# Order of statistics, scaling and stores at the end of a cross-attention and feed-forward kernel

## The chip, the cores and the metric

The kernel runs on one core of a Trainium2 chip. The metric is the device time of one execution in microseconds (us). Engines are called by the profile's names: PE is TensorE (matrix products), DVE is VectorE, ACT is ScalarE, POOL is GpSimd, SP is SyncE, which here only issues transfers. SBUF is the core's working memory, PSUM the memory of eight banks that PE writes its products to.

## The reference

The inputs are x (4 batches of 2048 tokens, 512 features, fp32), a context of 77 keys for each batch, two gates and the weights. Cut to what matters:

```python
x = x + tanh(g_xattn) * (softmax(q(layernorm(x)) @ k.T / 8) @ v @ Wo + bo)   # 16 heads
x = x + tanh(g_ffn) * (layernorm(x) @ W[idx] + b[idx])                        # idx chosen by argmax
```

The second line concerns us here. The product of a centred weight with the not yet normalized row is scaled afterwards by the row's 1/sqrt(var + eps), so the norm's statistics are needed only when the product is scaled, not before it is made. The result is y plus bias plus scaled product.

## The kernel before

The 8192 tokens are worked in 16 groups of 512. For each group there are scores, softmax, the attention's product (`at`), a residual sum in columns (features on partitions), a change of layout to rows of y, and the feed-forward product `ff`. Each 512 x 512 product is made in seven block products instead of eight (class `Seven`): `product(s)` issues the matmuls of step s into one of three PSUM banks, `post(s)` copies the bank to the SBUF tile `snap` (ACT, L467) or adds it there (DVE, L486). Sums of column blocks that these products read (`T1` to `T4`, `Columns.sum`) are made on POOL (L432).

The schedule is manual: each engine works its instructions in the order in which the code issues them, and waits between engines come from the data they share. The tracking goes by whole banks in PSUM.

In rows, a group's y is a tile of 128 partitions x 16 row blocks x 128 features. `stats` makes statistics of it on DVE (L365), `gather` has ACT bring them to 32 partitions in 8 copies (L374), half of them to PSUM (`ps_st`), `calc` works the variance out in seven DVE instructions (L381 to L388), `power` takes it to the power -1/2 on POOL (L393), and `back` copies the result to all four quarters of the partitions as `rs` (L398).

The last group has no later work to hide behind, so it is worked in halves and quarters. The last four of its 128-feature columns of blocks are named by two indices: `h` is the half of the features, `v` the half of the tokens (rows 8v to 8v+7 of y). `n1` holds the statistics of tokens half v=1 (the second half), `n0` those of v=0 (the first). Each quarter of the product goes through the same steps: finished in `snap` (or, for h=1, v=0, left in the bank `ff.ps[0]`), transposed to rows in the tile `t` by two DVE transposes (`f_rows`, `to_rows`, L412), scaled by `rs` (L996 on ACT block by block, L1000 at once on DVE or POOL), and added to y (L1004). The bias is added to y by halves on POOL (`half_bias`, L991). `store` (L594) writes half the tokens by four transfers of 128 KB, on the queues it is given.

In the loop over the last product's steps, s is the step: after step 3 quarter (h, v) = (0, 1) is complete, after step 4 (1, 1), after step 5 (0, 0), after step 6 (1, 0). The order before, by engine, behind the last attention product: DVE makes rows and statistics for v=1, the last rows of x, `n1.calc`, rows and statistics for v=0, then the adds and transposes of step 3, `n0.calc`, and so on; the four copies `n0.back` are on DVE:

```python
            n0.back(nc.vector.tensor_copy)
            scaled_at_once(0, 0, n0.rs, nc.gpsimd)
            added(0, 0, nc.gpsimd)
```

PSUM tiles come from `bank()`, a pool of seven buffers; the statistics have the eighth bank, `stat`.

Of the kernel before, what the change touches and what calls it, by code (L numbers as in the profile page):

```python
# [11 lines left out]
ALU = mybir.AluOpType  # L12
# [7 lines left out]
def flamingo_block_kernel(  # L20
# [33 lines left out]
    nc = tc.nc  # L54
# [9 lines left out]
    NA = 4  # L64
# [10 lines left out]
    NG = T // 32  # L75
# [12 lines left out]
    def bank(name):  # L88
        return pm.tile([P, 512], F32, tag="mm", name=name)
# [22 lines left out]
    stat = pst.tile([P, 512], F32, tag="st", name="ps_st")  # L112
# [19 lines left out]
    def row_tile(name):  # L132
        return wp.tile([P, NG, P], F32, tag="row", name=name, bufs=3)
# [9 lines left out]
    t = wp.tile([P, NK * T + KH * T2], F32, tag="pT", name="wq")  # L143
# [3 lines left out]
    xg, ys, ts_ = {}, {}, {}  # L147

    def rows_of(t, i):
        return t[ts(i, T), :].rearrange("(g c) d -> c g d", c=32)  # L150
# [91 lines left out]
    def gather():  # L242
        t = row_tile("wfr").rearrange("p g j -> p (g j)").rearrange("p (c d) -> p c d", c=NDC)
        for c in range(NDC):
            at = bass.IndirectOffsetOnAxis(ap=rows_u[:, c : c + 1], axis=0)
            nc.gpsimd.indirect_dma_start(out=t[:, c, :], out_offset=None, in_=W, in_offset=at)
        at = bass.IndirectOffsetOnAxis(ap=rows_u[:, NDC:], axis=0)
        nc.gpsimd.indirect_dma_start(out=bf_r, out_offset=None,
                                     in_=b.rearrange("o (a j) -> (o a) j", j=P), in_offset=at)
        nc.gpsimd.tensor_scalar(bo_c, bo_c, tgx, None, ALU.mult)  # L250
        nc.gpsimd.tensor_scalar(bf_r, bf_r, tgf, None, ALU.mult)
        return t
# [100 lines left out]
    class Norms:  # L353
# [10 lines left out]
            for g in range(g0, g0 + n):  # L364
                nc.vector.bn_stats(self.s6[:, at + g, :], t[:, g, :])  # L365

        def gather(self):

            self.mean = stat[:32, : 8 * self.n].rearrange("p (n e) -> p n e", e=2 * NA)
            self.m2 = small.tile([32, self.n, 2 * NA], F32, tag="m2", name="m2")  # L370
            parts = self.s6.rearrange("p g (h s) -> p g h s", h=2)
            for a in range(NA):
                for to, k in ((self.mean, 1), (self.m2, 2)):
                    nc.scalar.copy(to[:, :, ts(a, 2)], parts[ts(a, 32), :, :, k])  # L374
# [34 lines left out]
    def to_rows(dst, cols, q, v=None):  # L409

        g = slice(0, NG) if v is None else ts(v, NG // 2)
        nc.vector.transpose(dst[:, g, ts(q, 32)], cols.rearrange("p (g c) -> p g c", c=32))  # L412
# [81 lines left out]
    norms, xc, yc, sc, pT = ({} for _ in range(5))  # L494
# [51 lines left out]
    def p_columns(i, k0, k1):  # L546
        for k in range(k0, k1):
            if k == 0:
                t = wp.tile([P, NK * T + KH * T2], F32, tag="pT", name="pT")
                pT[i] = Columns(t[:, : NK * T].rearrange("p (n t) -> p n t", t=T),  # L550
                                T1=t[:, NK * T :].rearrange("p (n t) -> p n t", t=T2))
            nc.vector.transpose(pT[i].all[:, k, :].rearrange("p (g h r) -> p g h r", h=HA, r=R),  # L552
                                key_chunk(sc[i], k))

    def residual(j, at, which, engine=None):

        c = xc[j].at["B" + which]
        (engine or nc.gpsimd).tensor_tensor(c, c, at.quarter(which), ALU.add)  # L558

    def residual_last(j, at):  # L560

        c = xc[j].at["B21"]
        for n, pair in enumerate(at.pairs):
            q = pair + NDC // 2
            nc.vector.scalar_tensor_tensor(c[:, n, :], at.ps[0][:, n, :], bo_c[:, q : q + 1], c[:, n, :],
                                           ALU.add, ALU.add)

    def y_rows(j, q0, v=None):
        if j not in ys:
            ys[j] = row_tile("y")  # L570
        for q in (q0, q0 + 1):
            c = xc[j].all[:, q, :]
            to_rows(ys[j], c if v is None else c[:, ts(v, T2)], q, v)

    def f_rows(f, ff, half, v=None):
        if f not in ts_:
            ts_[f] = row_tile("t")
        for n in range(2):
            to_rows(ts_[f], ff.chunk(half, n, v), 2 * half + n, v)

    def add_bias(f, engine):
        engine.tensor_tensor(ys[f], ys[f], bf_r.unsqueeze(1).to_broadcast([P, NG, P]), ALU.add)
# [9 lines left out]
    def store(f, g0=0, n=NG, queues=(nc.sync,)):  # L592
        for a in range(NA):
            queues[a % len(queues)].dma_start(out=rows_of(out, f)[:, ds(g0, n), ts(a, P)],  # L594
                                              in_=ys[f][ts(a, 32), ds(g0, n), :])
# [54 lines left out]
    ff = None  # L650

    def end_of_ff(f):
        ff.product(6)
        ff.post(6)
# [11 lines left out]
    n = norms[0]  # L666
# [67 lines left out]
    e = (8, 16, 24, 32, 41, 50, 57)  # L734
# [47 lines left out]
    for i in range(1, NGRP):  # L782
        j, f, nx = i - 1, i - 2, i + 1
        n = norms[i]
# [67 lines left out]
        for s in range(7):  # L852
# [12 lines left out]
            if 1 <= s:  # L865
                e = (0, 10, 20, 32, 44, 56, 64)
# [44 lines left out]
        ff = Seven("ps_f", w_ffn, yc[j], (0, 1), SNAP)  # L911
        for s in range(6):
# [16 lines left out]
            if 2 <= s:  # L929
                k = (0, 2, 3, 5, 6)  # L930
# [5 lines left out]
    j, f = NGRP - 1, NGRP - 2  # L936
    n = norms[NGRP] = Norms(NGRP)
    n1, n0 = Norms(NGRP + 1, NG // 2), Norms(NGRP + 2, NG // 2)
# [3 lines left out]
    for s in range(7):  # L942
        at.product(s)
        if s == 0:
            at.post(0)
            end_of_ff(f)
            p_columns(j, 6, 10)
            f_rows(f, ff, 1)
            pT[j].sum("T2")
            pT[j].sum("T3")  # L950
            n.stats(ys[f], 0, 0, NG)
        if s == 1:
            n.gather()
            add_bias(f, nc.vector)
        if s == 2:
            n.calc()
            pT[j].sum("T4")
            n.power()
        if s == 3:
            n.back()  # L960
            f_scale(f, n.rs, 0, 8)
        if s == 4:
            residual(j, at, "12")
            f_scale(f, n.rs, 8, 8)
        if 0 < s < 6:
            at.post(s)
        if s == 4:
            f_add(f, 0, NG, nc.vector)
            store(f)
        if s == 5:  # L970
            residual(j, at, "22")
            y_rows(j, 0, 1)
        if s == 6:
            yc[j].sum("T3")
            residual(j, at, "11")
            y_rows(j, 2, 1)
            n1.stats(ys[j], -8, 8, 8)
            n1.gather()
            y_rows(j, 0, 0)
            residual_last(j, at)  # L980
    yc[j].sum("T1")
    yc[j].sum("T2")
    ff = Seven("ps_f", w_ffn, yc[j], (0, 1), SNAP, None, Seven.BY_TOKENS)

    def by_feature(t, h, v):

        return t[:, ts(v, NG // 2), ts(h, D // NA // 2)]

    def half_bias(v, engine):
        y = ys[j][:, ts(v, NG // 2)]  # L990
        engine.tensor_tensor(y, y, bf_r.unsqueeze(1).to_broadcast([P, NG // 2, P]), ALU.add)  # L991

    def scaled(h, v, rs):
        d = by_feature(ts_[j], h, v)
        for g in range(NG // 2):
            nc.scalar.activation(d[:, g, :], d[:, g, :], AF.Copy, scale=rs[:, g : g + 1])  # L996

    def scaled_at_once(h, v, rs, engine):
        d = by_feature(ts_[j], h, v)
        engine.tensor_tensor(d, d, rs.unsqueeze(2).to_broadcast(list(d.shape)), ALU.mult)  # L1000

    def added(h, v, engine):
        y = by_feature(ys[j], h, v)
        engine.tensor_tensor(y, y, by_feature(ts_[j], h, v), ALU.add)  # L1004

    for s in range(6):
        ff.product(s)
        if s == 0:
            half_bias(1, nc.gpsimd)
            n1.calc()  # L1010
            n1.power()
            y_rows(j, 2, 0)
            n0.stats(ys[j], 0, 0, 8)
            yc[j].sum("T4")
            half_bias(0, nc.gpsimd)
        ff.post(s)
        if s == 2:
            n1.back()
            n0.gather()
        if s == 3:  # L1020
            f_rows(j, ff, 0, 1)
            scaled(0, 1, n1.rs)
            n0.calc()
            n0.power()
        if s == 4:
            f_rows(j, ff, 1, 1)
            scaled(1, 1, n1.rs)
            added(0, 1, nc.gpsimd)
        if s == 5:
            f_rows(j, ff, 0, 0)  # L1030
            n0.back(nc.vector.tensor_copy)
            scaled_at_once(0, 0, n0.rs, nc.gpsimd)
            added(0, 0, nc.gpsimd)
    ff.product(6)
    for k in range(2):
        to_rows(ts_[j], ff.ps[0][:, k, :], 2 + k, 0)
    added(1, 1, nc.vector)
    store(j, 8, 8, (nc.sync, nc.sync, nc.sync, nc.scalar))
    scaled_at_once(1, 0, n0.rs, nc.vector)
    added(1, 0, nc.vector)  # L1040
    store(j, 0, 8, (nc.sync, nc.scalar))


# [39 lines left out]
```

## Time and profile before

| what | us |
|---|---|
| median of 3 runs (lowest, highest) | 1262.63 (1260.26, 1262.82) |
| the profiled execution | 1261.98 |
| its span, first to last instruction | 1260.2 |
| PE busy in the span | 1241.3 (99%) |
| DVE busy | 914.0 (73%) |
| POOL busy | 876.8 (70%) |
| ACT busy | 685.6 (54%) |
| PE's last matmul ends | 1249.89 |
| DVE's last add (L1004) ends | 1254.82 |

The span is what the profile's clock covers; the 1.8 us between it and the execution's time lie around it. Busy time is an average over the whole kernel, and the change is in its last 23 us. For them the timeline is read: each line has the start, the length, the engine, the line of the code, the operation with output and inputs, and in brackets how long the engine was idle before it and what ended that.

### The profile page before, as it was taken

What the parts mean: (1) busy time and instruction counts of PE and PEld (TensorE: products, weight loads), DVE (VectorE), ACT (ScalarE), POOL (GpSimd) and SP (SyncE); (2) the same over time, 40 slices, a digit from 0 to 9 for tenths busy, and PEclk for the clock granted to TensorE, in tenths of its full rate; (3) what the DMA queues carried; (4) which work ended last, traced back from release to release, by engine and by line L of the source; (5) the groups of instructions that cost most, each with busy time, mean ns of one, the idle gap of its engine ahead of it and who ended that gap; (6) DMA issues with size and microseconds to landing.
All of it is one profiled execution on the core that took longest, in us unless ns stands there. A gap on an engine that the chain in (4) does not pass through costs nothing.

```text
span 1260.2 us, 16984 instructions
## 1 busy us (share of the span) xinstructions
PE 1241.3 (99%) x5704; PEld 1061.0 (84%) x5704; DVE 914.0 (73%) x1859; ACT 685.6 (54%) x1964; POOL 876.8 (70%) x470
## 2 busy tenths in 40 slices
PE   9989999999999999999999999999999999999996
PEld 6665888888888888888888888888888888888885
DVE  5778876677776767777776877666777876666577
ACT  3547473827456483736548373654738274564823
POOL 4332896685967778584968778575986877585766
PEclk9999999999999999999999999999999999999998
DMA  9775500304006030303206030122304111010102
GB/s 254 293 214 179 147 1 1 68 21 116 15 1 151 1 68 1 67 1 93 58 1 151 1 67 1 26 42 84 67 1 109 43 43 25 1 34 1 34 1 67
DMA packets 95221, 80.27 MB, mean 64 GB/s; under 512 B 3856, under 2 KB 83088, under 8 KB 95136
## 3 DMA queue, kind: packets, MB, share of 16 engines
q1 hardware_dynamic: 92768, 76.74, 23.8%
q0 software_dynamic: 608, 1.13, 0.4%
q10 hardware_dynamic: 1760, 1.34, 0.3%
q8 instruction: 45, 0.74, 0.2%
q14 instruction: 40, 0.33, 0.1%
HBM read 44.07 MB, written 35.13 MB: 63 GB/s over the span
## 4 chain that ended last, share of the span: by engine, by line
PE 93%; POOL 3%; DVE 2%; ACT 1%; DMA 1%; issue 0%; SPq 0%; POOLq 0%; DVEq 0%; ACTq 0%
PE ps_s L461 36%; PE ps_a L461 36%; PE ps_f L461 15%; PE ps_kv L266 2%; PE ps_vo L331 2%; PE ps_m L296 2%; POOL vo L123 1%; DMA xg<-in_x_dram 1%; POOL pT L432 1%; PE ps_w L167 0%; POOL s L543 0%; DVE snap L486 0%; POOL xc L558 0%; ACT wf L644 0%; POOL wf L123 0%
## 5 line engine op out<-in xcount | busy, mean ns | idle before, releaser
L461 PE MATMUL ps_a<-pT,vo 128*128 128x256 f32 x2240 | 486.2, 379 | 0.0
L461 PEld LDWEIGHTS ps_a<-pT,vo 128*128 128x128 f32 x2240 | 425.6, 190 | 57.9
L532 ACT ACTIVATE s<-s,nmx,up 128x77 f32<-128x77 f32 x1024 | 355.6, 446 | 1.0 <-DVE nmx L526 1.0
L432 POOL TENSOR_TENSOR pT<-pT 128x1280 f32<-128x1280 f32 x64 | 185.8, 2905 | 171.5 <-PE ps_a L461 162.0
L461 PE MATMUL ps_s<-tq,m 128*128 128x256 f32 x1280 | 292.4, 381 | 6.5 <-ACT snap L467 5.6
L461 PEld LDWEIGHTS ps_s<-tq,m 128*128 128x128 f32 x1280 | 243.3, 191 | 43.9 <-ACT snap L467 6.4
L467 ACT COPY snap<-ps_s 128x512 f32<-128x512 f32 (+1 forms) x188 | 93.3, 514 | 289.2 <-DVE t L412 131.3
L461 PE MATMUL ps_s<-xc,m 128*128 128x256 f32 x960 | 222.3, 381 | 0.0
L461 PEld LDWEIGHTS ps_s<-xc,m 128*128 128x128 f32 x960 | 182.6, 191 | 29.3 <-DVE vo L334 2.4
L543 POOL TENSOR_TENSOR s<-s,sm 128x1232 f32<-128x1232 f32 x64 | 145.2, 2270 | 64.0 <-DVE sm L540 41.6
L486 DVE TENSOR_TENSOR snap<-snap,ps_s 128x512 f32<-128x512 f32 (+1 forms) x141 | 83.5, 593 | 123.5 <-PE ps_s L461 120.7
L461 PE MATMUL ps_f<-tq,wf 128*128 128x256 f32 x512 | 118.5, 379 | 0.6 <-DVE snap L486 0.4
L552 DVE STREAM_TRANSPOSE pT<-s 128x512 f32<-128x512 f32 x160 | 101.0, 678 | 18.2 <-POOL s L543 18.2
L393 POOL TENSOR_TENSOR r<-r,neghalf 32x16 f32<-32x16 f32 (+1 forms) x33 | 93.1, 2831 | 29.6 <-DVE r L388 29.1
L432 POOL TENSOR_TENSOR tq<-xc,tq 128x512 f32<-128x512 f32 x64 | 85.3, 1333 | 34.8 <-PE ps_f L461 32.3
L461 PEld LDWEIGHTS ps_f<-tq,wf 128*128 128x128 f32 x512 | 97.1, 190 | 14.5 <-issue 0.7
L515 DVE STREAM_TRANSPOSE s<-snap 128x512 f32<-128x512 f32 x156 | 99.8, 685 | 10.1 <-ACT snap L467 7.9
L539 DVE TENSOR_REDUCE sm<-s 128x16 f32<-128x1232 f32 x64 | 91.5, 1430 | 20.8 <-ACT s L532 20.7
L524 DVE TENSOR_REDUCE ps_st<-s 128x16 f32<-128x1232 f32 x64 | 92.4, 1444 | 2.1
L432 POOL TENSOR_TENSOR tq<-xc 128x512 f32<-128x512 f32 x64 | 81.4, 1272 | 13.7 <-DVE xc L407 12.3
L461 PE MATMUL ps_f<-xc,wf 128*128 128x256 f32 x384 | 90.7, 379 | 0.0
L467 ACT COPY snap<-ps_f 128x512 f32<-128x512 f32 x63 | 36.9, 585 | 88.9 <-PE ps_f L461 88.8
(126 smaller groups left out, 1180.3 us busy)
## 6 DMA issues: line engine op xcount, KB each, us to landing
xg<-in_x_dram SPq DMA_DIRECT2D x64, 256.0 KB, 6.2
out_dram<-y SPq DMA_DIRECT2D x60, 256.0 KB, 4.1
vo<-vo_d SPq DMA_DIRECT2D x16, 640.0 KB, 5.5
vo_d<-vo SPq DMA_DIRECT2D x16, 512.0 KB, 3.8
m<-m_d SPq DMA_DIRECT2D x12, 640.0 KB, 4.1
m_d<-vo SPq DMA_DIRECT2D x4, 960.0 KB, 6.1
wq<-in_WqT_dram SPq DMA_DIRECT2D x8, 256.0 KB, 8.0
wq<-in_Wo_dram SPq DMA_DIRECT2D x1, 2048.0 KB
```

Source lines behind the costliest of these rows:

```text
L266: nc.tensor.matmul(ps[:, :n], w[:, c, ts(p, P)], keys[:, c].rearrange("p b j -> p (b j)"), start=(c == 0), stop=(c == NCC - 1))
L393: nc.gpsimd.tensor_tensor(r, r, neghalf[:32, : r.shape[1]], ALU.pow)
L432: (engine or nc.gpsimd).tensor_tensor(self.at[name], self.at[a], self.at[b_], op)
L461: nc.tensor.matmul(self.ps[r][:, n, :], self.w(blk, c, pair), self.cols(cname, c), start=(first and n == 0 and c == 0), stop=(c == h - 1), ...
L467: nc.scalar.copy(dst, self.ps[r])
L486: nc.vector.tensor_tensor(c, c, self.ps[r], ALU.add)
L515: nc.vector.transpose(key_chunk(sc[i], k), cols.rearrange("p (g h r) -> p g h r", h=HA, r=R))
L524: nc.vector.tensor_reduce(mx, head(i, h), AX.X, ALU.max)
L532: nc.scalar.activation(head(i, h)[:, g, :], head(i, h)[:, g, :], AF.Exp, scale=norms[i].up[:, g : g + 1], bias=nmx[h][:, g : g + 1])
L539: nc.vector.tensor_reduce(sm, head(i, h), AX.X, ALU.add)
L543: nc.gpsimd.tensor_tensor(head(i, h), head(i, h), sums[h].unsqueeze(2).to_broadcast([P, NG, J]), ALU.mult)
L552: nc.vector.transpose(pT[i].all[:, k, :].rearrange("p (g h r) -> p g h r", h=HA, r=R), key_chunk(sc[i], k))
```

## The change

Five things change, all in the last group:

1. The rows of y for the first half's second features and the statistics `n0.stats` come directly behind the last residual sum, ahead of `n1.calc`. `n0.gather` comes one step earlier (ahead of ACT's copy of step 2) and writes a bank of its own, `ps_n`; `n0.calc` and `n0.power` follow `n1`'s.
2. On POOL, `T4` goes ahead of `n1.power`, and the bias of the first half behind `n0.power`.
3. Quarter (1, 1) is transposed into a new PSUM bank `ps_r` instead of `t`; half of its blocks are scaled there at once by DVE, the other half by four ACT instructions. Quarter (1, 0) is transposed into another such bank and scaled there at once by DVE. The adds to y read the bank.
4. `n0.back` is on ACT, behind the scaling of quarter (1, 1). The add of quarter (0, 1) on POOL is issued one step earlier.
5. The second half is added to y and its stores issued before the last quarter is transposed; its four transfers alternate between SP and ACT (before: three on SP, one on ACT).

```diff
-        def gather(self):
-            self.mean = stat[:32, : 8 * self.n].rearrange("p (n e) -> p n e", e=2 * NA)
+        def gather(self, bank_=stat):
+            self.mean = bank_[:32, : 8 * self.n].rearrange("p (n e) -> p n e", e=2 * NA)
...
             residual_last(j, at)
+            y_rows(j, 2, 0)
+            n0.stats(ys[j], 0, 0, 8)
...
+    def rows_bank(chunks):
+        d = bank("ps_r").rearrange("p (g j) -> p g j", g=NG // 2)
+        for k in range(2):
+            nc.vector.transpose(d[:, :, ts(k, 32)], chunks[k].rearrange("p (g c) -> p g c", c=32))
+        return d
+
+    def scaled(d, rs, g1=NG // 2):
+        for g in range(g1):
             nc.scalar.activation(d[:, g, :], d[:, g, :], AF.Copy, scale=rs[:, g : g + 1])
+    def scaled_at_once(d, rs, engine, g0=0):
+        d, rs = d[:, g0:], rs[:, g0:]
         engine.tensor_tensor(d, d, rs.unsqueeze(2).to_broadcast(list(d.shape)), ALU.mult)
+    def added(h, v, d, engine):
         y = by_feature(ys[j], h, v)
+        engine.tensor_tensor(y, y, d, ALU.add)

     for s in range(6):
         ff.product(s)
         if s == 0:
             half_bias(1, nc.gpsimd)
+            yc[j].sum("T4")
             n1.calc()
             n1.power()
-            y_rows(j, 2, 0)
-            n0.stats(ys[j], 0, 0, 8)
-            yc[j].sum("T4")
-            half_bias(0, nc.gpsimd)
+        if s == 2:
+            n0.gather(bank("ps_n"))
+            n0.calc()
+            n0.power()
         ff.post(s)
         if s == 2:
             n1.back()
-            n0.gather()
+            half_bias(0, nc.gpsimd)
         if s == 3:
             f_rows(j, ff, 0, 1)
-            scaled(0, 1, n1.rs)
-            n0.calc()
-            n0.power()
+            scaled(by_feature(ts_[j], 0, 1), n1.rs)
+            added(0, 1, by_feature(ts_[j], 0, 1), nc.gpsimd)
         if s == 4:
-            f_rows(j, ff, 1, 1)
-            scaled(1, 1, n1.rs)
-            added(0, 1, nc.gpsimd)
+            r1 = rows_bank([ff.chunk(1, k, 1) for k in range(2)])
+            scaled_at_once(r1, n1.rs, nc.vector, NG // 4)
+            scaled(r1, n1.rs, NG // 4)
+            n0.back()
         if s == 5:
             f_rows(j, ff, 0, 0)
-            n0.back(nc.vector.tensor_copy)
-            scaled_at_once(0, 0, n0.rs, nc.gpsimd)
-            added(0, 0, nc.gpsimd)
+            t = by_feature(ts_[j], 0, 0)
+            scaled_at_once(t, n0.rs, nc.gpsimd)
+            added(0, 0, t, nc.gpsimd)
     ff.product(6)
-    for k in range(2):
-        to_rows(ts_[j], ff.ps[0][:, k, :], 2 + k, 0)
-    added(1, 1, nc.vector)
-    store(j, 8, 8, (nc.sync, nc.sync, nc.sync, nc.scalar))
-    scaled_at_once(1, 0, n0.rs, nc.vector)
-    added(1, 0, nc.vector)
+    added(1, 1, r1, nc.vector)
+    store(j, 8, 8, (nc.sync, nc.scalar))
+    r0 = rows_bank([ff.ps[0][:, k, :] for k in range(2)])
+    scaled_at_once(r0, n0.rs, nc.vector)
+    added(1, 0, r0, nc.vector)
     store(j, 0, 8, (nc.sync, nc.scalar))
```

In the changed kernel the scaling at once is L1008, ACT's scaling L1004, the transposes into a bank L999, the adds L1012 and the bias L993.

More of the change, by code (lines that the diff above doesn't have):

```diff
@@ L991, in half_bias @@
         engine.tensor_tensor(y, y, bf_r.unsqueeze(1).to_broadcast([P, NG // 2, P]), ALU.add)
-    def scaled(h, v, rs):
-        d = by_feature(ts_[j], h, v)
-        for g in range(NG // 2):
+    def rows_bank(chunks):
[5 more added lines that the diff above has]
+        for g in range(g1):
             nc.scalar.activation(d[:, g, :], d[:, g, :], AF.Copy, scale=rs[:, g : g + 1])
-    def scaled_at_once(h, v, rs, engine):
-        d = by_feature(ts_[j], h, v)
+    def scaled_at_once(d, rs, engine, g0=0):
+        d, rs = d[:, g0:], rs[:, g0:]
         engine.tensor_tensor(d, d, rs.unsqueeze(2).to_broadcast(list(d.shape)), ALU.mult)
-    def added(h, v, engine):
+    def added(h, v, d, engine):
         y = by_feature(ys[j], h, v)
-        engine.tensor_tensor(y, y, by_feature(ts_[j], h, v), ALU.add)
+        engine.tensor_tensor(y, y, d, ALU.add)
     for s in range(6):
```

## The prediction, made before the changed kernel ran

> **What bounds the kernel now.** I began with the page's busy shares and its chain of waits: TensorE (PE) carries 93% of the chain, and the change touches no product. So the change can only pay after the last matmuls, and I went to the timeline of the last 25 us, then to the chain, the waits and the DMA view of that stretch.
>
> The page's chain line, by engine:
>
> ```profile
> PE 93%; POOL 3%; DVE 2%; ACT 1%; DMA 1%; issue 0%; SPq 0%; POOLq 0%; DVEq 0%; ACTq 0%
> ```
>
> The timeline of the end (start, length, engine, line, operation):
>
> ```profile
> 1240.51 0.62 DVE L388 TENSOR_SCALAR r<-tot 32x8 f32<-32x8 f32 x1
> ...
> 1247.03 0.16 DVE L388 TENSOR_SCALAR r<-tot 32x8 f32<-32x8 f32 x1
> ...
> 1247.33 1.64 POOL L393 TENSOR_TENSOR r<-r,neghalf 32x8 f32<-32x8 f32 x1 [0.92 <-DVE r L388]
> ...
> 1247.92 1.97 PE L461 MATMUL ps_f<-tq,wf 128*128 128x256 f32 x8 [0.37 <-DVE snap L486]
> ...
> 1249.88 0.88 DVE L398 COPY rs<-r 32x8 f32<-32x8 f32 x4
> 1250.79 0.78 DVE L412 STREAM_TRANSPOSE t<-ps_f 128x256 f32<-128x256 f32 x2
> 1250.84 1.04 POOL L1000 TENSOR_TENSOR t<-t,rs 128x512 f32<-128x512 f32 x1 [0.63 <-DVE rs L398]
> 1251.50 0.93 DVE L1004 TENSOR_TENSOR y<-y,t 128x512 f32<-128x512 f32 x1
> 1251.96 1.59 POOL L1004 TENSOR_TENSOR y<-y,t 128x512 f32<-128x512 f32 x1
> 1252.35 1.75 DVE L1000 TENSOR_TENSOR t<-t,rs 128x512 f32<-128x512 f32 x1
> 1252.51 3.27 ACTq L594 DMA_DIRECT2D out_dram<-y  x3
> 1254.13 0.69 DVE L1004 TENSOR_TENSOR y<-y,t 128x512 f32<-128x512 f32 x1
> ```
>
> PE ends at 1249.89, and for 4.9 us more VectorE (DVE) works without a gap: from 1247.2 on it sets the end. Its last add ends at 1254.82; the span ends at 1260.2. Three things stretch that DVE chain: four copies of `rs` (0.88), the add of 0.93 and the scaling of 1.75, where the same shape at 1254.13 took 0.69. Both long ones end together with a POOL instruction plus 0.55: POOL's scaling (L1000) ends at 1251.88, DVE's add at 1252.43; POOL's add ends at 1253.55, DVE's scaling at 1254.10. They waited for POOL. So did L388: 0.62 beside POOL's bias add (until 1241.11), 0.16 with POOL idle.
>
> **What the skill says.** The Trainium skill, "SBUF — State Buffer", section "Who interferes with whom": a DVE instruction with two SBUF inputs, or a copy or tensor_scalar in a two-port mode, locks itself and GpSimd out of each other, the later one waiting for the whole of the earlier. The trace agrees: 1.75 and 0.93 against 0.69, 0.62 against 0.16. "VectorE: DVE Perf Modes", "Why PSUM operands drop a tier": an fp32 operand in PSUM keeps DVE out of the two-port mode. I conclude that adds and scalings with one operand in PSUM run past POOL; L486 (SBUF and PSUM in) took 0.65 to 0.69 with POOL busy beside it. "ScalarE: Activation LUTs", "Step-by-step: what each stage is for": a PSUM destination is the quicker one for ScalarE (ACT). The gathers agree, 172 ns against 207:
>
> ```profile
> L374 ACT COPY m<-s 32x16 f32<-32x16 f32 x8 | 1.7, 207 | 0.0
> L374 ACT COPY ps_st<-s 32x16 f32<-32x16 f32 x8 | 1.4, 172 | 6.2 <-DVE s L365 6.1
> ```
>
> **The change, part by part.** Times "after" are estimates, built from durations and pitches of this trace.
>
> *Statistics moved forward.* DVE's residual pieces end at 1239.17. Now the two y transposes (0.75) and eight statistics (1.65) come here, to 1241.64, and only then `n1.calc` (1.57, as the undisturbed one at 1245.62 took), to 1243.15 instead of 1241.13. `n1` is 2.0 later; its first user, the scaling on ACT, waited for a transpose at 1245.70 anyway. ACT gathers `n0` (1.36) by 1243.03, into a bank of its own, so it does not wait for `n1.calc`. ACT's copy of the third product is queued behind: 1243.65 instead of 1243.00; the fifth product, which overwrites that bank, began at 1243.94. Slack 0.3, cost nothing; if it is short, PE slips by as much and the fifth product's add has another 0.4.
> `n0.calc` follows at once: start 1243.1, 1.57, but its L388 falls into POOL's power for `n1` (1243.23 to 1244.88, 1.65), and if that locks as the bias add did, it ends at 1244.9 instead of 1244.7. The idle 0.72 that DVE had at 1243.5 is filled.
>
> *POOL's queue.* `T4` (1.26) goes ahead of the power and is done at 1242.4, early enough for the last product. Then without a gap: power `n1` to 1244.88, power `n0` (from 1244.98) to 1246.62, bias add of the first half (2.35) to 1248.97, the add of quarter 0,1 (1.26) to 1250.24. The bias add was at 1244.06 before: it is moved behind both powers and pushes what follows. Scaling of quarter 0,0 (1.04) and its add (1.26 clear; 1.59 before, as DVE stood in its way), with 0.08 between, close POOL's work.
>
> *DVE.* From 1244.85: add, two transposes, add, two transposes at the pitch seen at 1247.11 to 1249.95 (1.39 a set), to 1247.7. PE's last product waits for the second add (1246.9 instead of 1247.78), so its wait of 0.37 goes and PE ends at about 1249.35. New: scaling half of quarter 1,1 in PSUM, 256 columns. A PSUM destination costs 12 ns in the nearest rows (L385 220, L386 208); L486 took 420 for 256 columns, 650 to 690 for 512. I take 0.42 and later 0.68. That gives 1248.16, the sixth product's add and transposes 1249.54. Then adding quarter 1,1 (0.69), transposing the last quarter (0.78), scaling (0.68), adding (0.69). The `rs` copies (0.88) have gone to ACT, the two blocks (0.38 and 1.07) are gone.
>
> *ACT.* Copies of `rs` for `n1` by 1245.75; eight scalings from 1246.36 (2.02) to 1248.38; four in PSUM, each waiting for the one before: 0.25 each if they overlap as the eight did, 0.33 if not, so done by 1249.3 to 1249.65; `rs` for `n0` (0.82) by 1250.15 to 1250.5. Before, 1250.76.
>
> *Who is last.* POOL's scaling starts 0.08 after those copies, at 1250.25 to 1250.6, and POOL ends at 1252.6 to 1252.95. DVE adds quarter 1,1 at 1249.6 to 1249.9 and ends at 1252.4 to 1252.7. So **POOL takes over from DVE as the last engine**, at about 1252.8: 2.0 earlier than 1254.82.
>
> *Stores.* The DMA view of 1254.8 to 1261, busy tenths in 40 slices of 0.155 us:
>
> ```profile
> DMA  8898406888888878999998510000000000000000
> ```
>
> The gap in the sixth slice, at 1255.6, is the end of the first set of four transfers; the second ends in the 24th, at 1258.5. Counted from the add that released it, the first set (1252.43) took 3.2 and the second (1254.82) 3.7. After: second half out at 1250.5, first half at 1252.8, 2.3 apart where it was 2.4, so the sets should stay apart. Both have two transfers on SP and two on ACT; before, the first set had three and one. I carry 3.7 over. On ACT the stores stand behind nothing but the `rs` copies.
>
> *Unknown costs.* Transposing into PSUM: not in the trace. From PSUM it took what it takes from SBUF (428 against 424 ns a piece). I take 0.39 pitch; below, nothing to gain but 0.05; above, I allow twice that. Two sets lie on DVE, which has 0.2 slack: at twice, +1.4. Scaling in PSUM: at worst POOL still blocks it (1.75), +0.9. L388 not blocked: -0.1. ACT's four scalings decide 0.35. New banks: seven buffers, six others in use or free long before, no wait seen in the queue's order; at most 0.3.
>
> **Sum.** Against the profiled execution (1261.98, of which 1260.2 is span and 1.8 lies around it): 1254.82 - 1252.8 = 2.0, so a span of 1258.2 and 1260.0 in all. That execution was 0.65 under the median of 1262.63; from the median, **1260.6**. A fifth of a per cent, 2.5 us, is about what a measurement of this kernel can tell from no change: three runs of it spread over 2.6.
>
> **The rivals.**
> *A, as above:* gain 1.7 to 2.3. For it: POOL's queue is closed from 1243.23 on, 9.4 us of work that nothing in the change shortens. Chance 0.55.
> *B, stores land sooner as well.* The last set took 3.7, the first 3.2. The last may do it in 3.2 too, with less of the other ahead of it on SP's queue; with the cheap ends of ACT and L388: 2.0 + 0.5 + 0.2 = 2.7, so 1259.9. Against: the last set had two and two already. Chance 0.31.
> *C, the end moves little.* PSUM transposes at twice their price, or scaling still blocked: 2.0 - 1.2 = 0.8, so 1261.8. Against: PSUM cost 12 ns wherever it shows. Chance 0.09.
> *D, slower: transposing into PSUM is slow.* Four such pieces lie on DVE's path, two before ACT's scaling and so before POOL's last work. With 0.2 slack, break-even is where four cost 2.2 more, 0.94 a piece instead of 0.39. At 1.6 a piece, 4 x 1.2 - 0.2 = 4.6 lost against 2.0 won: 1265.2. For it: no row shows a transpose written to PSUM. Against: reading costs nothing extra, and the writes of L384, L385 cost 12 ns. Chance 0.05.
>
> **Numbers.** A and the spread of the runs (medians of three move by about 1) put over 2.5 in some 40% of A's cases: 0.22; B gives 0.28; together faster 0.50. Within 0.2%: the rest of A, B and nearly all of C, 0.44. Slower 0.06: D and a little of C. The range goes from B with its landing and a low median (2.7 + 1.0 under 1262.63, 1258.9) up to C with a high one (1262.4).
>
> **What would show it.** In the profile after: DVE's L1008 of 512 columns near 0.68 and its adds near 0.69, none near 1; `L388` of `n0` near 0.4; POOL without a gap from 1243.2 and last, near 1252.8, just behind DVE; the first stores out at 1250.5; PE's last product without its wait. It is wrong if transposes into `ps_r` are clearly over 0.4 a piece, if POOL waits over 0.5 for `rs`, if the sets of stores overlap, or if PE ends later than 1249.9.

## The result, and the profile after

| | before | after |
|---|---|---|
| median of 20 runs | 1262.62 us | 1259.97 us |
| lowest to highest | 1260.26 to 1263.50 | 1258.03 to 1261.41 |
| profiled execution, its span | 1261.98, 1260.2 | 1260.11, 1258.3 |

The ratio is 0.9979 (95% interval 0.9973 to 0.9986): 2.65 us faster, just over the 0.2% that the prediction set as the bound for "faster", with an interval of about 1.8 to 3.4 us.

The page's chain, by engine, after:

```profile
PE 90%; DVE 4%; POOL 3%; ACT 1%; DMA 1%; issue 1%; SPq 0%; DVEq 0%; POOLq 0%; ACTq 0%
```

DVE carried 2% before. In order of time, the chain before left PE at 1244.11, inside the last feed-forward product. Now it leaves PE at 1211.77, goes by ACT, DVE and POOL through the group ahead, and stays in DVE from 1234.52 to the last add. From there on DVE has no gap left in which it would wait for PE, ACT or POOL. PE is close behind, though: DVE's second add of the product (L486 at 1246.33) began 0.04 after the matmuls that it reads had ended by the profile (1244.40 + 1.89 = 1246.29; these ends are modelled). So work taken off DVE ahead of that add should gain next to nothing; no run tried it.

The timeline of the end (start, length, engine, line, operation, and in brackets the idle time before with what ended it):

```profile
1243.33 0.16 DVE L388 TENSOR_SCALAR r<-tot 32x8 f32<-32x8 f32 x1
...
1243.56 3.25 POOL L393 TENSOR_TENSOR r<-r,neghalf 32x8 f32<-32x8 f32 x2 [0.76 <-DVE r L388]
...
1244.84 0.16 DVE L388 TENSOR_SCALAR r<-tot 32x8 f32<-32x8 f32 x1
...
1246.33 0.68 DVE L486 TENSOR_TENSOR snap<-snap,ps_f 128x512 f32<-128x512 f32 x1
...
1247.05 0.95 DVE L999 STREAM_TRANSPOSE ps_r<-snap 128x256 f32<-128x256 f32 x2
...
1247.86 1.89 PE L461 MATMUL ps_f<-tq,wf 128*128 128x256 f32 x8
1248.11 0.43 DVE L1008 TENSOR_TENSOR ps_r<-ps_r,rs 128x256 f32<-128x256 f32 x1
...
1248.58 1.25 ACT L1004 ACTIVATE ps_r<-ps_r,rs 128x64 f32<-128x64 f32 x4
...
1249.75 0.80 ACT L398 COPY rs<-r 32x8 f32<-32x8 f32 x4
1249.93 0.69 DVE L1012 TENSOR_TENSOR y<-y,ps_r 128x512 f32<-128x512 f32 x1
1250.53 0.96 DVE L999 STREAM_TRANSPOSE ps_r<-ps_f 128x256 f32<-128x256 f32 x2
1250.63 1.04 POOL L1008 TENSOR_TENSOR t<-t,rs 128x512 f32<-128x512 f32 x1 [0.27 <-DVE y L1012]
1250.69 3.38 ACTq L594 DMA_DIRECT2D out_dram<-y  x4
1251.60 0.70 DVE L1008 TENSOR_TENSOR ps_r<-ps_r,rs 128x512 f32<-128x512 f32 x1
1251.75 1.26 POOL L1012 TENSOR_TENSOR y<-y,t 128x512 f32<-128x512 f32 x1
1252.40 0.69 DVE L1012 TENSOR_TENSOR y<-y,ps_r 128x512 f32<-128x512 f32 x1
```

Executions differ in when the feed-forward product begins (1237.03 in the kernel before, 1237.49 here, 1238.45 in experiment e5 below), although nothing ahead of it was changed. So from here on I count **from the first matmul of the last `ff`**. On that clock DVE's last add ends at 15.60 instead of 17.79, POOL's at 15.52 instead of 16.52, PE's last matmul at 12.26 instead of 12.86, the span at 20.81 instead of 23.17. I call this stretch, from the first `ff` matmul to the span's end, the tail. It is 2.36 us shorter; the medians moved by 2.65, and the interval of that contains 2.36.

Every add and scaling of 512 columns on DVE now takes its plain length, 0.69 or 0.70, with POOL busy beside it. The bracket at POOL's scaling names DVE, but ACT's `rs` copies (1249.75 + 0.80 = 1250.55) and DVE's add (1250.62) ended almost together. What POOL needs are the copies: here and in e3, e7 and e12, below, its scaling starts 0.08 after them, and in e12 0.01 before DVE's add had ended.

The DMA view of 1252.8 to 1259, again 40 slices of 0.155:

```profile
DMA  7899999789889888889999852000000000000000
```

The last digit is in the 25th slice; the GB/s row of the same view has a last small entry, 13, in the 26th, and the last packet of the trace ends at 1256.80. That is 3.7 after the last add, the same as before (1258.52, also 3.7). The dip in the eighth slice, at 1253.9, is about where the second set takes over. By the packets of each queue the sets overlap a little: ACT's queue finishes its half of the first set at 1254.25, 0.3 after SP's queue began the second. The first set took 3.6 from its add, where it had taken 3.2.

### The profile page after: what moved, and what is told of

It is laid out like the page before. It is cut to its first block, busy times and chain, and to the rows that moved or that the text cites. A ratio compares the mean times of both kernels' runs of the same rounds, so it can differ in the third digit from the quotient of the medians.

```text
span 1258.3 us, 16987 instructions
## 1 busy us (share of the span) xinstructions
PE 1240.9 (99%) x5704; PEld 1060.5 (84%) x5704; DVE 915.1 (73%) x1856; ACT 685.2 (54%) x1964; POOL 876.8 (70%) x470
## 4 chain that ended last, share of the span: by engine, by line
PE 90%; DVE 4%; POOL 3%; ACT 1%; DMA 1%; issue 1%; SPq 0%; DVEq 0%; POOLq 0%; ACTq 0%
PE ps_s L461 36%; PE ps_a L461 34%; PE ps_f L461 14%; PE ps_kv L266 2%; PE ps_vo L331 2%; PE ps_m L296 1%; POOL vo L123 1%; DVE s L365 1%; DMA xg<-in_x_dram 1%; POOL pT L432 1%; PE ps_w L167 0%; DVE snap L486 0%; ACT t L586 0%; POOL s L543 0%; POOL xc L558 0%
## 5 line engine op out<-in xcount | busy, mean ns | idle before, releaser
L486 DVE TENSOR_TENSOR snap<-snap,ps_s 128x512 f32<-128x512 f32 (+1 forms) x141 | 83.5, 593 | 122.8 <-PE ps_s L461 120.1
```

The costliest lines, as they stand in the source:

```text
L486: nc.vector.tensor_tensor(c, c, self.ps[r], ALU.add)
```

## The experiments

All times are on the clock just introduced; ratios are against the kernel before, with 95% intervals. The kernels differ by less than the scatter of a kernel's executions, so the profile's tail carries the argument and the ratio only bounds it. The two middle columns are of one execution each; e4, e5 and e11, which leave the work ahead of the last add as it is, give 15.60 again.

| kernel | last add | span's end | ratio |
|---|---|---|---|
| before | 17.79 | 23.17 | |
| after | 15.60 | 20.81 | 0.9979 (0.9973 to 0.9986) |
| e1 rows in SBUF | 18.29 | 23.54 | 1.0008 (1.0000 to 1.0017) |
| e2 last quarter in PSUM | 16.72 | 22.08 | 0.9997 (0.9988 to 1.0005) |
| e7 statistics as before | 16.74 | 22.05 | 0.9989 (0.9981 to 0.9998) |
| e10 statistics alone | 17.56 | 22.94 | 0.9998 (0.9990 to 1.0006) |
| e12 quarter (1,1) in SBUF | 16.20 | 21.35 | 0.9982 (0.9975 to 0.9989) |
| e3 one statistics bank | 16.50 | 21.75 | 0.9992 (0.9983 to 1.0000) |
| e4 store order in the code | 15.60 | 20.85 | 0.9981 (0.9973 to 0.9989) |
| e11 first half stored first | 15.60 | 22.88 | 0.9996 (0.9988 to 1.0005) |
| e5 stores three and one | 15.60 | 20.85 | 0.9984 (0.9977 to 0.9991) |
| e6 fused | 15.76 | 20.98 | 0.9986 (0.9980 to 0.9993) |

### e1: everything but PSUM

```diff
-        d = bank("ps_r").rearrange("p (g j) -> p g j", g=NG // 2)
+        d = by_feature(ts_[j], 1, chunks[2])     # rows in the SBUF tile t
```

The two callers add the half of the tokens, 1 or 0, to the list as `chunks[2]`.

> The change with its quarters (1,1) and (1,0) transposed into the SBUF tile t and scaled there; order, statistics and stores as changed. Measure: from the first ff matmul to the end of the last add, 17.79 us before and 15.60 after. Theory (an operand in PSUM keeps DVE out of POOL's way): the scaling of 256 columns waits for POOL's bias add, near 1.4 instead of 0.43, one add or the last scaling waits for POOL once or twice more, ACT's rs copies slip by about 0.8; the measure is 17.2 to 18.0, the gain of the change gone. Rival (the forward move of the statistics is what gains, PSUM is only a place): transposes 0.09 a piece cheaper, measure 15.2 to 15.6.

Measured 18.29, 0.29 above the range of the theory, and a longer tail than before. The timeline of e1:

```profile
1246.87 2.35 POOL L993 TENSOR_TENSOR y<-y,bf_r 128x1024 f32<-128x1024 f32 x1
...
1248.00 2.73 DVE L1008 TENSOR_TENSOR t<-t,rs 128x256 f32<-128x256 f32 x1
1249.19 1.25 POOL L1012 TENSOR_TENSOR y<-y,t 128x512 f32<-128x512 f32 x1
...
1253.49 0.69 DVE L1008 TENSOR_TENSOR t<-t,rs 128x512 f32<-128x512 f32 x1
1253.68 1.62 POOL L1012 TENSOR_TENSOR y<-y,t 128x512 f32<-128x512 f32 x1
1254.29 1.56 DVE L1012 TENSOR_TENSOR y<-y,t 128x512 f32<-128x512 f32 x1
```

The scaling of 256 columns, 0.43 in the bank, took 2.73. I had expected it to wait for the bias add alone. It waited for that and for the add that stood right behind it on POOL (until 1250.44), and then worked for 0.3. The last add took 1.56 beside POOL's last one. The last quarter's scaling, in SBUF here as in the kernel before, took 0.69: it began ahead of POOL's add, and this time POOL's add was the longer one (1.62, alone 1.26). So scaling in SBUF is not slow in itself. The rival, which would have had this kernel at 15.2 to 15.6, falls.

### e2: PSUM for the last quarter alone

```diff
+    r0 = bank("ps_r").rearrange("p (g j) -> p g j", g=NG // 2)
     for k in range(2):
-        to_rows(ts_[j], ff.ps[0][:, k, :], 2 + k, 0)
+        nc.vector.transpose(r0[:, :, ts(k, 32)], ff.ps[0][:, k, :].rearrange("p (g c) -> p g c", c=32))
...
-    scaled_at_once(1, 0, n0.rs, nc.vector)
-    added(1, 0, nc.vector)
+    nc.vector.tensor_tensor(r0, r0, n0.rs.unsqueeze(2).to_broadcast(list(r0.shape)), ALU.mult)
+    nc.vector.tensor_tensor(by_feature(ys[j], 1, 0), by_feature(ys[j], 1, 0), r0, ALU.add)
```

> The kernel before with one edit: quarter (1,0) transposed into a PSUM bank and scaled there. Theory (blocking): DVE's last scaling 0.70 instead of 1.75, two transposes 0.18 dearer, the add of 0.93 stays blocked since quarter (1,1) is still in SBUF; DVE ends about 0.9 earlier, measure 16.8 to 17.0 against 17.79. Rival (the 1.75 is not a wait for POOL): scaling stays near 1.7, measure 17.9.

Measured 16.72, 0.08 under the range of the theory: 1.07 off the end by this one edit of the kernel before. In its timeline:

```profile
1252.44 1.59 POOL L1004 TENSOR_TENSOR y<-y,t 128x512 f32<-128x512 f32 x1
1252.84 0.68 DVE L1040 TENSOR_TENSOR ps_r<-ps_r,rs 128x512 f32<-128x512 f32 x1
```

The same scaling that took 1.75 takes 0.68, although POOL's add runs beside it from beginning to end. The 1.75 was a wait for POOL.

### e7 and e10: the statistics' part taken out, and alone

e7 is the changed kernel with the old order of statistics; e10 the kernel before with the new order and `gather` taking its bank as in the change. The edit in e10, reversed in e7:

```diff
             residual_last(j, at)
+            y_rows(j, 2, 0)
+            n0.stats(ys[j], 0, 0, 8)
...
+            yc[j].sum("T4")
             n1.calc()
             n1.power()
-            y_rows(j, 2, 0)
-            n0.stats(ys[j], 0, 0, 8)
-            yc[j].sum("T4")
-            half_bias(0, nc.gpsimd)
+        if s == 2:
+            n0.gather(bank("ps_n"))
+            n0.calc()
+            n0.power()
         ff.post(s)
         if s == 2:
             n1.back()
-            n0.gather()
+            half_bias(0, nc.gpsimd)
         if s == 3:
             f_rows(j, ff, 0, 1)
             scaled(0, 1, n1.rs)
-            n0.calc()
-            n0.power()
```

> The change with the first half's rows and statistics, their gathering, powers, T4 and bias add put back into the old order (one statistics bank); PSUM quarters, rs copies on ACT and store order as changed. If the parts add up, the measure is 16.6 to 16.9 (before 17.79, after 15.60): about 1.0 from PSUM and the rs copies, 1.2 from the statistics, POOL ends last because its power for n0 still comes behind the bias add. If the statistics' move gains nothing, 15.6; if it is everything, 17.8.

> The kernel before with only the statistics' part of the change: first half's rows and statistics forward, gathered into a bank of their own, n0.calc and both powers early, T4 ahead, bias add of the first half behind the powers. Quarters stay in SBUF, rs copies of n0 on DVE. Measure: from the first ff matmul to the end of the last add (before 17.79, after 15.60, changed without PSUM 18.29). Theory (moved without PSUM, the bias add on POOL now stands beside DVE's two-input and copy instructions): DVE's rs copies wait for POOL until near 12.9, the last add, scaling and add wait once each; measure 17.8 to 18.4, no gain. Rival (idle time filled and statistics off DVE's end gain by themselves): about 0.7 of idle and more of calc leave the end, measure 16.4 to 16.9.

e7 measured 16.74, inside the range, but not by adding up: e10 brings far less than the 1.2 that the expectation gave the statistics. In e7's timeline ACT stands idle until DVE comes to the quarter's scaling, because DVE makes `n0.calc` first:

```profile
1250.48 1.25 ACT L1002 ACTIVATE ps_r<-ps_r,rs 128x64 f32<-128x64 f32 x4 [1.51 <-DVE ps_r L1006]
...
1252.53 1.04 POOL L1006 TENSOR_TENSOR t<-t,rs 128x512 f32<-128x512 f32 x1 [1.12 <-DVE y L1010]
```

e10 measured 17.56, 0.24 under the theory's range, and far from the rival's 16.4 to 16.9. Its power for `n0` is over at 9.3 (1247.18), but:

```profile
1249.48 1.26 POOL L1006 TENSOR_TENSOR y<-y,t 128x512 f32<-128x512 f32 x1
1249.84 1.45 DVE L398 COPY rs<-r 32x8 f32<-32x8 f32 x4
...
1252.88 1.75 DVE L1002 TENSOR_TENSOR t<-t,rs 128x512 f32<-128x512 f32 x1
```

The four copies (0.88 before) wait for POOL's add, and the scaling waits as it always had. So the parts do not add up: the statistics alone bring 0.23, the rest alone 1.05, both 2.19. Moving the statistics clears DVE's end, and POOL's moved instructions then stand where DVE's copies and two-input instructions are. The time stayed cleared only in the kernels that have the last quarter in PSUM and these copies on ACT; e1, with the copies on ACT alone, lost it. What the copies' move is worth with PSUM in place was not tested. Without the statistics' move it shows nothing: e7, which has both banks, the copies on ACT and the order of the stores, is at 16.74, no better than e2 with the last quarter's bank alone (16.72).

### e12: which of the two quarters

```diff
-            r1 = rows_bank([ff.chunk(1, k, 1) for k in range(2)])
-            scaled_at_once(r1, n1.rs, nc.vector, NG // 4)
-            scaled(r1, n1.rs, NG // 4)
+            f_rows(j, ff, 1, 1)
+            r1 = by_feature(ts_[j], 1, 1)
+            scaled(r1, n1.rs)
```

> The change with quarter (1,1) transposed into SBUF and scaled there by ACT alone, eight times; the last quarter stays in PSUM. Theory: ACT's scaling ends near 13.0 from the first ff matmul instead of 12.3, its rs copies for n0 at 13.85 instead of 13.05, POOL's scaling and add slip with them and end last near 16.3; DVE saves its scaling of 0.43 and waits for ACT instead; measure 16.2 to 16.5. Rival 1 (only the last quarter's place counts): 15.5 to 15.7. Rival 2 (the add of quarter (1,1), two SBUF inputs, is shut out by POOL for a whole instruction or two): 17 or more.

Measured 16.20, the lower end of the range. As the theory had it, ACT is late, and both others wait for it:

```profile
1250.69 0.69 DVE L1012 TENSOR_TENSOR y<-y,t 128x512 f32<-128x512 f32 x1 [0.99 <-ACT t L1004]
...
1251.37 1.04 POOL L1008 TENSOR_TENSOR t<-t,rs 128x512 f32<-128x512 f32 x1 [0.84 <-ACT rs L398]
```

The add of quarter (1,1) with both inputs in SBUF took its plain 0.69, since POOL stood idle waiting for the same engine; rival 2 falls. So the first `ps_r` bank is worth 0.6, by letting DVE take half of ACT's scaling; in SBUF DVE's half was shut out (2.73 in e1). e12 takes away the bank and the sharing together. The last quarter's bank is worth its unblocked scaling (e2).

### e3: the bank of its own

```diff
-            n0.gather(bank("ps_n"))
+            n0.gather()
```

> The change with n0 gathered into the same bank as n1. Theory (whole-bank tracking makes the gather wait for n1.calc): gather starts near 6.1 after the first ff matmul instead of 4.5, ACT's copy of the third product is 1.4 to 1.6 later, the fifth product waits about 1.2, n0.calc and POOL's second power slip by 1.4 to 1.6; measure 17.0 to 17.3. Rival (n1.calc is over by then, the bank buys little): measure 15.6 to 15.9.

Measured 16.50, between the two ranges: the bank is worth 0.9 of the 2.19. In its timeline:

```profile
1243.24 0.17 ACT L374 COPY ps_st<-s 32x16 f32<-32x16 f32 x1 [1.35 <-DVE dv L386]
...
1245.14 1.99 PE L461 MATMUL ps_f<-tq,wf 128*128 128x256 f32 x8 [0.42 <-ACT snap L467]
```

The mechanism is the expected one; its size was overstated. The gather starts behind L386, the last instruction that reads the bank, not behind the whole of `n1.calc` (5.59 after the first `ff` matmul, not 6.1); the fifth product slips by 0.6 (7.49 instead of 6.91), of which the profile calls 0.42 a wait, not by 1.2.

### e4, e11, e5: the stores

```diff
     added(1, 1, r1, nc.vector)
-    store(j, 8, 8, (nc.sync, nc.scalar))
...
     added(1, 0, r0, nc.vector)
+    store(j, 8, 8, (nc.sync, nc.scalar))      # e4: here
     store(j, 0, 8, (nc.sync, nc.scalar))
+    store(j, 8, 8, (nc.sync, nc.scalar))      # e11: here
```

> The change with the second half's stores issued behind the last add, ahead of the first half's. Last add stays at 15.6 from the first ff matmul. Theory (1 MB leaves at the rate seen): from the last add to the span's end 6.7 to 7.4 us instead of 5.2, so 1.5 to 2.2 slower. Rival (the landing is mostly a fixed delay, storing the second half first buys little): 5.2 to 5.7.

> The change with the two sets of stores exchanged in the queues: the first half's, which waits for the last add, ahead of the second half's. In e4 the queues' order stayed as it was, so it tested nothing; here SP and ACT hold the second half back behind the first. Last add stays at 15.6 from the first ff matmul. Theory (1 MB then leaves after the last add at 200 to 250 GB/s): last add to the span's end 6.7 to 7.6 instead of 5.2, so the time is 1.5 to 2.4 longer. Rival (transfers mostly wait, their number counts little): 5.2 to 5.7.

e4 was a miss of mine: on SP and on ACT nothing stands between the places, so the order in each queue stayed the same and the stores still went out behind DVE's first add. It serves as a second execution of the change: 15.60 and 20.85. In e11 the queues do hold the second half back. The DMA view of 1250 to 1260.3, slices of 0.26:

```profile
DMA  0000000000000005888879999899999842000000
```

Nothing moves before 1253.9; the 1 MB is out by 1258.8, and the span ends 7.28 after the last add instead of 5.21. So the half megabyte costs 2.1 us where it is not hidden, as the theory had it. The kernel before hid it too: its two adds end 2.4 apart (1252.43 and 1254.82), those of the changed kernel 2.5. So this part of the change keeps a gain and should add none; that was not tested alone.

e5 has three of the first set on SP and one on ACT, as before.

> The change with the second half's four transfers put three on SP and one on ACT, as before. Theory (the first set is over before the second begins): no difference, last add to span's end 5.1 to 5.3. Rival (two and two let the last set land sooner): 0.3 to 0.5 longer.

Measured: span's end 5.25 after the last add, against 5.21. No difference, so the rival falls. The reason given in the theory holds for e5 alone: there the first set is over 0.2 before the second begins, in the changed kernel they overlap by 0.3, and it costs nothing that shows (last packet 3.7 after the add in both).

### e6: one instruction in place of two

```diff
-    scaled_at_once(r0, n0.rs, nc.vector)
-    added(1, 0, r0, nc.vector)
+    y0 = by_feature(ys[j], 1, 0)
+    for g in range(NG // 2):
+        nc.vector.scalar_tensor_tensor(y0[:, g, :], r0[:, g, :], n0.rs[:, g : g + 1], y0[:, g, :], ALU.mult, ALU.add)
```

> The change with the last quarter's scaling and add (0.70 + 0.69 and a gap) replaced on DVE by eight scalar_tensor_tensor of 64 columns each, y = bank * rs + y. If one starts every 0.14 as L384 does on small tiles, DVE ends 0.3 to 0.4 earlier; POOL then ends last, 15.5 from the first ff matmul, so the end gains 0.1 at most. If PSUM makes one 0.2 or more, DVE ends 0.1 to 0.3 later and the end with it.

```profile
1251.86 1.62 DVE L1049 SCALAR_TENSOR_TENSOR y<-ps_r,rs,y 128x64 f32<-128x64 f32 x8
```

One starts every 0.2, and eight take 1.62 where scaling and add took 1.49 with the gap between them. The end is 0.16 later, within the second forecast. Whether PSUM makes them slow was not tested. None of these versions beats the changed kernel: DVE is busy throughout and POOL ends 0.08 before it.

## Why the prediction was right, point by point

**The bound.** That only the stretch behind the last matmuls could pay, and that DVE set it by waiting for POOL, is shown by e2: the scaling loses the whole of the 1.07 counted as a wait (1.75 to 0.68). The pair of transposes cost 0.16 more there (0.94), and the add, still in SBUF, took 0.15 less (0.78), so these two cancel.

**Sum and size.** The prediction had DVE's last add at 1252.4 to 1252.7 and POOL's end at 1252.6 to 1252.95, which is 15.37 to 15.67 and 15.57 to 15.92 on the common clock. Measured: 15.60 and 15.52. Taken as 1252.8 or 15.77, the sum was 0.17 too late, and the span ended 5.2 after the last add instead of the 5.4 carried over. That is not a sooner landing, for the last packet ends 3.7 after the add in both; the difference lies behind the last packet (1.7 before, 1.5 after), and there the other runs scatter from 1.5 to 1.7. So the forecast of 2.0 was 0.36 short of the tail's 2.36 and 0.65 short of the medians; the median forecast was 1260.6, measured 1259.97. The span, 1258.2 forecast and 1258.3 measured, agrees better than the reasoning deserves: the profiled execution started its `ff` 0.46 later, which ate the difference.

**Who is last.** Wrong by a hair: DVE, by 0.08, not POOL. Two terms were mis-sized. The transposes into PSUM take 0.95 for two, not 0.78, and two such pairs are on DVE, 0.35 in all. The "12 ns" for a PSUM destination, on which the low price leaned, was read off two different operations (L385 and L386). And `L388` of `n0` was not blocked by POOL's power (0.16, inside POOL's 1243.56 to 1246.81): this gave DVE 0.2 and POOL 0.1 back. `n0.calc` also began 0.16 sooner on the common clock than forecast (5.91, not 6.07). That DVE's end fell inside its range is thus in part luck: 0.36 won and 0.35 lost.

**ACT's four scalings.** One every 0.32, the upper of the two values (0.33): none began before the one ahead of it had ended.

**Signs of being wrong.** Two of the four that the prediction named came, both small. The transposes into `ps_r` are over 0.4 a piece (0.46), and the sets of stores overlap, by 0.3: with two transfers on each queue the first set took 3.6, not the 3.2 of three and one. The first cost the 0.35 above, the second nothing that shows. POOL did wait for `rs`, but 0.27 and not over 0.5, so its queue was not closed to the end; and PE ended sooner, as forecast (12.26, forecast 12.32).

**Statistics' move.** Priced as idle time filled and POOL's queue pushed back. The price of the new bank was put at "at most 0.3" as a risk; its worth was not priced at all, and e3 shows it as 0.9. Nor did the prediction say that the two parts need each other; e7 and e10 show that 0.9 of the 2.19 comes from neither part alone.

**Rivals.** B, stores landing sooner (3.2 instead of 3.7): refuted by the profile after (3.7 again) and by e5. More than half of the forecast's "faster" (0.28 of 0.50) rested on it. The measured 2.65 is nearer to B's 2.7 than to A's 1.7 to 2.3, but B's cause is not there; what came is A, with a tail 0.36 shorter than forecast and an unexplained 0.3 on top, and that this lands just beyond 0.2% is in part luck. C and D: PSUM transposes cost 0.09 a piece more, not 0.39 or 1.2; both fall. The measured 0.21% has an interval that reaches to both sides of the bound of 0.2%.

What stays open: whether the remaining 0.3 between tail and medians is anything but scatter, and what the move of the `rs` copies to ACT brings by itself. No run here tells it.

## What to carry to other kernels

Read each duration against the same shape elsewhere in the trace. One that is longer, and ends a fixed time after another engine's instruction, is likely a wait for that engine, though the profile shows it as work; and the cure can be where the operand lies, not when the instruction runs. Test the parts of a change alone and taken out: here 0.2 and 1.05 made 2.2, because clearing DVE's queue put POOL's instructions in its way. Before changing the order of instructions in the code, look at what stands between them in that engine's own queue; if nothing does, nothing changes.

## What the runs showed of the hardware that was not expected

- A DVE instruction with two SBUF inputs waited through two POOL instructions in a row (2.73 us in e1): POOL's second began at the end of the first, ahead of the DVE instruction that had waited for 1.2 us. It does not always go so. In the kernel before, at 329.10, a DVE sum of two SBUF inputs (L123) waited for POOL too, but then went first, and POOL's next instruction took 2.52 where it takes 1.27 alone. What decides is open.
- POOL's power did not hold DVE's tensor_scalar L388 up (0.16), while POOL's bias add did (0.60 and 0.61 in e2 and e7, 0.62 before). The trace of the kernel before shows that it is the power that differs, and not L388: L123, with two inputs of 1280 columns in SBUF, took 1.45 inside the powers, 1.48 with POOL idle, and 2.50 beside POOL's other instructions (329.10). Why was not tried.

```profile
424.21 5.79 POOL L393 TENSOR_TENSOR r<-r,neghalf 32x16 f32<-32x16 f32 x2 [1.40 <-DVE r L388]
...
425.58 1.45 DVE L123 TENSOR_TENSOR vo<-vo 128x1280 f32<-128x1280 f32 x1
```

- A 32x32 block transpose of 128x256 written to PSUM takes 460 ns, to SBUF 424, whether it reads SBUF or PSUM (462 and 428 from PSUM); a pair takes 0.95 against 0.77. Elementwise, the destination hardly shows: L384 with the same inputs took 208 ns into SBUF and 210 into PSUM.
- ACT's scaling of 128x64 in place in PSUM takes 288 ns against 334 in SBUF. But in one bank none began before the one ahead had ended, 0.32 apart, while in SBUF they overlap, 0.24 apart.
